# First layer's opening in a written order: rows scaled in pairs on ScalarE, zeros later, routing and sends ahead of the first batch's convolutions

## The chip, the cores and the metric

The kernel runs on one core of a Trainium2 chip. A core has five engines that run their own instruction streams and wait for each other through semaphores: TensorE (PE in the profile; its weight loads are shown apart as PEld), VectorE (DVE), ScalarE (ACT), GpSimd (POOL) and SyncE (SP, which here only issues DMAs). Sixteen DMA engines move data between the off-chip memory and the on-chip memory. The metric is the device time of one execution in microseconds (us), the median of several runs.

## The reference, cut to what matters

The input is 8 batches of 512 rows of 256 numbers in float32, 4096 rows in all. There are two layers, each of the form "normalise, then add an attention-like part and a mixture of experts":

```
xn = layernorm(x)
x  = x + mamba(xn) + experts8_top1(xn)        # first layer
xn = layernorm(x)
x  = x + attention16(xn) + experts8_top2(xn)  # second layer
```

The part called mamba here projects xn to z, x, B, C and dt, makes dt = softplus(dt + bias), runs a 4-tap convolution with silu over x, B and C, runs a state-space recurrence in chunks of 128 rows, forwards and backwards in time (16 heads of 64 channels: 8 per direction), gates with silu(z), normalises and projects back. The first layer's experts: logits = xn·Wr + br, softmax over 8, each row goes to its best expert (relu(row·W1 + b1)·W2 + b2) and is scaled by that probability. The second layer has a latent attention with 16 heads of 16 and a top-2 mixture with limited capacity.

## The kernel before, in words

**Rows in (lines 379 to 403, `steps`, with `norm_and_project`, 128 to 157).** For each batch b of 512 rows (4 tiles of 128): SP asks for u; VectorE makes mean and variance of each tile (`bn_stats`, `bn_aggr`, lines 135 and 136), an inverse square root out of eleven small instructions (`rsqrt`, 162 to 169), and writes the scaled rows to xn (line 141). TensorE turns them (line 148, eight transposes of 128x128), ScalarE copies the result out of PSUM (line 149, twice 128x512), TensorE projects to 24 columns, 16 of dt and 8 logits (line 153, 16 matmuls), and VectorE copies these to proj (line 157). The transposed batch is stored to memory (`xtd`, line 379) and loaded again where the convolutions want it. Only two buffers hold u. In between, ScalarE's queue issues eight DMAs that write zeros into xd0 (line 122), the list of expert rows. Then follow softplus (lines 404 to 425, VectorE mostly), the first batch's convolutions, the decays and the first chunk's matrices. All this is written before `manual_schedule`, so that the framework puts it in an order of its own.

**The chunk loop (from line 1193).** 64 chunks: 8 per batch, four forwards and four backwards in turn. From here each engine takes its instructions exactly in the order in which the program writes them. A chunk does a segment matrix (`segments`, line 1043 on TensorE, exponentials on ScalarE), `pairs`, `weigh` (line 1075, one large VectorE product, once per chunk: a good marker), `inside`, `before`, `behind`, and it carries pieces of the next batch's projections (line 856) and convolutions (lines 865 to 874) and of the last batch's gate and output (line 1000).

**Filler steps.** Between these pieces the loop calls `fill`, which takes one step of a list of generators: four steps per chunk, one more in the first two chunks of each batch and in the last twelve. First comes `route0` (lines 428 to 481): softmax, best expert, ranks, slots, then 32 sends, each a GpSimd DMA that scatters the 128 rows of one tile to their slots in xd0 (line 473, two sends per step). It has 22 steps, all that chunks 0 to 4 offer. Then `blocks`, the first layer's expert matmuls: 39 blocks of 128 rows, 196 steps (weights fetched by GpSimd DMAs, line 539; matmuls in lines 587 and 608). When these are used up, `late` begins: it prepares the second layer. For each batch: `norm` (fetch the first layer's rows, add the experts' rows with an accumulating DMA, normalise in place on ScalarE, line 672, after a DMA at line 665 has stored the rows as they were), `turn` (transpose and project, lines 688 to 701 and 246 to 282) and, over groups of batches, `route` (top 2 and sends of 8-byte pairs, line 762). `norm` of a batch can only begin when the chunk loop has finished that batch.

**The end of the loop and the second layer.** After chunk 63 the last batch is gated, normalised and projected in a short stretch in which `fill` is called 16 times more. Then the attention runs in 128 steps (scores line 1468, exponentials 1483, transposes 1490, values 1499) with the second layer's experts between them; what is left of `late` runs in its first steps: one step ahead of it, four at the end of step 0 (`follow`, line 1594), four in each step from step 1 on.

**A stray DMA of the loop.** At the end of chunk 3 ScalarE's queue clears the second layer's table (`tab`, line 1241, elements of 8 bytes).

## Time and profile before

| | us |
|---|---|
| median of 3 runs | 2028.68 |
| the runs | 2027.3, 2028.68, 2041.08 |
| the profiled execution | 2044.14 |
| its span, first to last instruction | 2042.4 |
| proj of the last batch copied (line 157) | at 84.5 |
| first `weigh` done | at 142.6 |
| `weigh` of chunk 5, of chunk 6 begins | at 219.8, at 240.4 |
| first expert matmul (line 587) | at 232.5 |
| `weigh` of chunk 63 begins | at 1107.0 |
| first scores of the attention (line 1468) | at 1164.4 |

Over the whole span TensorE is busy 88%, VectorE 71%, ScalarE 57%, GpSimd 33%. The share hides that the stretches differ: in the second layer and in most of the chunk loop TensorE is busy nearly all the time at the full granted clock, at the beginning and around the change of layers it is not. The granted clock is the share of TensorE's full clock that the chip allowed in a stretch. A row of the table of stretches gives, for each engine, the busy time and in brackets the number of instructions.

### The profile page before, as it was taken

Reading aid. Unit: us, or ns where it says so; the run is one execution under the profiler, and the core shown is the slowest. Engines: PE = TensorE matmul, PEld = TensorE weight load, DVE = VectorE, ACT = ScalarE, POOL = GpSimd, SP = SyncE. Lnnn points to the kernel's source line nnn. Section 1 sums busy time; section 2 is a strip of 40 time slices with the busy share of each in tenths; the row PEclk is TensorE's granted clock in tenths of the full one; section 3 lists DMA queues with packets and bytes.
Section 4 is the critical chain, followed back from the end, with each engine's and each line's share of the span. In section 5 each row is a group of like instructions: output and inputs, shape, how many; then the busy total and the mean of one; then the engine's idle time right before and its main releaser. Section 6 shows DMA issues by size and latency. Waiting matters only on the chain.

```text
span 2042.4 us, 33668 instructions
## 1 busy us (share of the span) xinstructions
PE 1807.4 (88%) x11768; PEld 1219.7 (60%) x11768; DVE 1440.6 (71%) x3387; ACT 1163.6 (57%) x2552; POOL 680.2 (33%) x619
## 2 busy tenths in 40 slices
PE   4665699899999999997888878999999999999997
PEld 3423477676667777674455545666666666666654
DVE  4685476767667576776746448788888878787885
ACT  1143253544445454453543247888888878788886
POOL 0037465645646564553324442111111111111030
PEclk9987899999999999998888768999999999999999
DMA  8214765454645555446454323231313131314171
GB/s 247 83 42 67 175 209 163 161 182 149 201 161 189 173 171 184 161 133 160 123 156 134 101 79 100 44 105 44 105 45 103 46 98 41 104 40 112 37 136 52
DMA packets 146472, 245.88 MB, mean 120 GB/s; under 512 B 26333, under 2 KB 106079, under 8 KB 134400
## 3 DMA queue, kind: packets, MB, share of 16 engines
q1 hardware_dynamic: 103536, 122.94, 19.5%
q0 software_dynamic: 33392, 114.95, 19.5%
q10 hardware_dynamic: 9376, 5.84, 1.5%
q8 instruction: 94, 1.54, 0.3%
q14 instruction: 74, 0.61, 0.1%
HBM read 184.70 MB, written 59.90 MB: 120 GB/s over the span
## 4 chain that ended last, share of the span: by engine, by line
PE 35%; ACT 10%; DVE 5%; DMA 2%; issue 1%; SPq 0%; ACTq 0%; POOL 0%; DVEq 0%; POOLq 0%
PE p_ps L1490 8%; PE o_ps L1499 6%; ACT s L1483 6%; PE s_ps L1468 4%; PE e_hp L1318 4%; PE e_yp L1331 4%; ACT pT L1491 3%; PE qp L261 2%; DMA xr<-yt 1%; DVE s L1475 1%; DVE s L1473 1%; PE pj L856 1%; PE op L1000 1%; PE fin L1431 1%; PE vp L279 1%
## 5 line engine op out<-in xcount | busy, mean ns | idle before, releaser
L1473 DVE TENSOR_SCALAR s<-s_ps 128x512 f32<-128x512 f32 x512 | 317.8, 682 | 152.5 <-PE s_ps L1468 150.9
L1483 ACT ACTIVATE s<-s,ng 128x512 f32<-128x512 f32 x512 | 330.8, 717 | 0.0
L1475 DVE CUSTOM_DVE_ANT_0 s<-s,band 128x512 f32<-128x512 f32 x512 | 322.7, 684 | 0.0
L1491 ACT COPY pT<-p_ps 128x512 f32<-128x512 f32 x512 | 275.5, 588 | 75.0 <-PE p_ps L1490 68.2
L1490 PE MATMUL p_ps<-ident,s 128*128 128x128 f32 x2048 | 284.5, 282 | 24.2 <-ACT pT L1491 17.9
L1490 PEld LDWEIGHTS p_ps<-ident,s 128*128 128x128 f32 x2048 | 234.0, 143 | 99.5 <-ACT pT L1491 34.4
L1338 POOL DMA_INDIRECT x<-e_yo,slots x28 | 45.6, 1628 | 623.3 <-ACT e_yo L1337 623.3
L856 PE MATMUL pj<-xT,w_in 128*128 128x512 f32 x384 | 204.6, 660 | 16.6 <-DVE cv L869 9.9
L587 PEld LDWEIGHTS h_ps<-xdT,w 128*128 128x128 f32 x1248 | 150.3, 194 | 23.0 <-issue 22.0
L1468 PE MATMUL s_ps<-kT,qT 16*128 16x512 f32 x1024 | 156.9, 664 | 5.2 <-DMA qT<-qd 5.2
L587 PE MATMUL h_ps<-xdT,w 128*128 128x128 f32 x1248 | 153.9, 277 | 3.5 <-DMA w<-in_w_dram,w_idx 3.5
L1027 POOL TENSOR_TENSOR au<-da,half 128x512 f32<-128x512 f32 x64 | 77.0, 1203 | 226.6 <-DVE da L425 107.2
L869 DVE SCALAR_TENSOR_TENSOR cv<-pj,w_conv_w,cv 128x511 f32<-128x511 f32 (+2 forms) x192 | 143.0, 745 | 10.9 <-ACT cv L865 6.9
L608 PE MATMUL y_ps<-w,hT 128*128 128x256 f32 x624 | 147.5, 380 | 0.0
L608 PEld LDWEIGHTS y_ps<-w,hT 128*128 128x128 f32 x624 | 115.7, 190 | 31.9 <-issue 16.9
L856 PEld LDWEIGHTS pj<-xT,w_in 128*128 128x128 f32 x384 | 72.9, 207 | 102.2 <-issue 89.6
L1499 PE MATMUL o_ps<-pT,vt 128*32 128x256 f32 x2048 | 130.9, 396 | 0.1
L1318 PE MATMUL e_hp<-e_xdT,e_w 128*128 128x256 f32 x448 | 121.2, 393 | 8.6 <-ACT e_hT L1321 7.6
L1101 POOL TENSOR_TENSOR yT<-yT,ex 128x512 f32<-128x512 f32 (+1 forms) x48 | 58.6, 1220 | 208.3 <-DVE ex L1100 137.8
L1081 PE MATMUL yd<-mt,xdt 128*64 128x128 f32 x1024 | 76.7, 296 | 44.5 <-DVE mt L1075 44.5
L1331 PE MATMUL e_yp<-e_w,e_hT 128*128 128x256 f32 x448 | 113.5, 386 | 1.0 <-ACT e_hT L1321 1.0
L1499 PEld LDWEIGHTS o_ps<-pT,vt 128*32 128x32 f32 x2048 | 62.1, 113 | 87.2 <-issue 55.1
(296 smaller groups left out, 3080.3 us busy)
## 6 DMA issues: line engine op xcount, KB each, us to landing
ex<-exd SPq DMA_DIRECT2D x96, 128.0 KB
u<-in_u_dram SPq DMA_DIRECT2D x16, 512.0 KB
fr<-fdd SPq DMA_DIRECT2D x64, 128.0 KB
od<-os SPq DMA_DIRECT2D x28, 256.0 KB
e_w<-in_ei_dram SPq DMA_DIRECT2D x7, 1024.0 KB
e_w<-in_eo_dram SPq DMA_DIRECT2D x7, 1024.0 KB
xd<-xd SPq DMA_DIRECT2D x39, 129.0 KB
vd<-vt SPq DMA_DIRECT2D x16, 288.0 KB
```

The lines of the kernel that those rows point to most:

```text
L587: T.matmul(hp[:, i, :], w1[:, k * FF + f * P : k * FF + (f + 1) * P], xdT[:, k * P : (k + 1) * P], start=(k == 0), stop=(k == KC - 1),)
L608: T.matmul(yp, hT[f // 4][:, f % 4, :], w2[:, f * DM : (f + 1) * DM], start=(f == 0), stop=(f == FC - 1))
L856: T.matmul(pj, w_in[:, k, o * P : (o + 1) * P], self.xT[:, k, :], start=(k == 0), stop=(k == KC - 1))
L1318: T.matmul(hp, w1[:, k, f * P : (f + 1) * P], xdT[:, k, :], start=(k == 0), stop=(k == KC - 1))
L1331: T.matmul(yp, hT[:, f, c * P : (c + 1) * P], w2[:, f, :], start=(f == 0), stop=(f == FC - 1))
L1468: T.matmul(sp[i], self.q[r, cols], self.k[r, :], start=True, stop=True)
L1473: V.tensor_scalar(self.p[i], sp[i], -CLAMP, CLAMP, ALU.max, ALU.min)
L1475: V.tensor_tensor_reduce(out=self.p[i], in0=self.p[i], in1=band[:, at : at + S], scale=1.0, scalar=-3.0e38, op0=ALU.mult, op1=ALU.max, acc ...
L1483: A.activation(self.p[i], self.p[i], AF.Exp, bias=self.ng[:, i : i + 1])
L1490: T.transpose(pp[:, k, :], self.p[i][:, k * P : (k + 1) * P], ident)
L1491: A.copy(pT[i][:, :, cc * P : (cc + 1) * P], pp)
L1499: T.matmul(op[32 * i : 32 * i + 32, half * 2 * P : (half + 1) * 2 * P], self.v[:, k, h * (AD + 1) : h * (AD + 1) + 32], pT[i][:, k, :], st ...
```

## The change

The opening moves into the hand-written order, and its parts are put in another sequence.

- All of u is asked for at once, into buffers that are free until later; the batches are taken in pairs, 2 and 3 first, 0 and 1 last, so that the transposed batches 0 and 1 stay on chip and are neither stored nor loaded.
- A pair's 8 tiles share one `rsqrt`. The rows are scaled on ScalarE (`activation` with Identity, a scale and a bias per row) and proj is copied by ScalarE, both on VectorE before.
- The zeros are issued from SP's queue in the second pair, no longer from ScalarE's queue from the first batch on. A row of xd0 and xn is 272 numbers wide, not 258.
- softplus takes a fused instruction per coefficient, where there were two.
- All of `route0` (now 39 steps, one send per step) runs ahead of the loop: the choice of slots before softplus is finished, nine sends before the decays, the other 23 between the first batch's convolution pieces. The loop's filler steps begin with `blocks`.
- w_out is loaded in chunk 2 and scaled in chunk 3. The stray clearing of `tab` stays at the end of chunk 3.
- In `norm` the store of the rows is issued ahead of the statistics (for the last batch already in `output`); in the attention the four steps at the end of step 0 are dropped.

```diff
-DW = DM + 2
+DW = DM + 16
...
-    us = {}
-
-    def ask(b):
-        us[b] = m1.tile([P, TPB, DM], FP, name="u", tag="u", bufs=2)
-        Y.dma_start(out=us[b], in_=rows_of(t["u"], b))
-
-    ask(0)
+    us = []
+    order = [*range(2, B), 0, 1]
+
+    def ask():
+        pool, tag, bufs = ((m1, "z", 1), (m2, "yT", 2), (m2, "yT", 2), (m2, "bc", 2))[len(us)]
+        both = pool.tile([P, HC, S], FP, name=tag, tag=tag, bufs=bufs).rearrange("p k s -> p (k s)")
+        us.append(both.rearrange("p (t d) -> p t d", d=DM))
+        for k in range(2):
+            Y.dma_start(
+                out=us[-1][:, k * TPB : (k + 1) * TPB, :], in_=rows_of(t["u"], order[2 * len(us) - 2 + k])
+            )
+
+    ask()
     w_small = load("w_small", [P, KC, 2 * NH + NE], l0c)
-    ask(1)
+    ask(), ask(), ask()
...
+    def rows_in():
+
+        G2 = 2 * TPB
+        for u, b0 in zip(us, order[::2]):
+            both = (b0, b0 + 1)
+            mv = r0p.tile([P, G2, 2], FP, name="mv", tag="mv")
+            for i in range(G2):
+                st = r0p.tile([P, 6], FP, name="st", tag="st", bufs=4)
+                V.bn_stats(st, u[:, i, :])
+                V.bn_aggr(mv[:, i, :], st)
+            ve = r0p.tile([P, G2], FP, name="ve", tag="ve")
+            V.tensor_scalar(ve, mv[:, :, 1], EPS, None, ALU.add)
+            rs = rsqrt(r0p, ve, [P, G2])
+            nm = r0p.tile([P, G2], FP, name="nm", tag="nm")
+            V.scalar_tensor_tensor(nm, mv[:, :, 0], -1.0, rs, ALU.mult, ALU.mult)
+            for i in range(G2):
+                A.activation(
+                    xn[:, b0 * TPB + i, :DM], u[:, i, :], AF.Identity,
+                    bias=nm[:, i : i + 1], scale=rs[:, i : i + 1],
+                )
+            if b0 == order[0]:
                 Y.dma_start(out=w_in, in_=t["w_in"])
...
+            if b0 == order[2]:
+                n = NBLK // B + 1
+                for k in range(B):
+                    lo, hi = k * n, min(NBLK, (k + 1) * n)
+                    Y.dma_start(
+                        out=xd0.rearrange("(p r) d -> p r d", p=P)[:, lo:hi, :],
+                        in_=bc(blank, 1, [P, hi - lo, DW]),
+                    )
+            xTs = {}
+            for b in both:
+                xTs[b] = m2.tile([P, KC, S], FP, name="xT", tag="xT")
+                for k in range(KC):
+                    tp = bank("tp", [P, S], 0)
+                    for c in range(TPB):
+                        T.transpose(tp[:, c * P : (c + 1) * P], xn[:, b * TPB + c, k * P : (k + 1) * P], ident)
+                    A.copy(xTs[b][:, k, :], tp)
+            for b in both:
+                pp = bank("pp", [P, TPB, 2 * NH + NE], 1)
+                for c in range(TPB):
+                    for k in range(KC):
+                        T.matmul(
+                            pp[:, c, :], xTs[b][:, k, c * P : (c + 1) * P], w_small[:, k, :],
+                            start=(k == 0), stop=(k == KC - 1),
+                        )
+                A.copy(proj[:, b * TPB : (b + 1) * TPB, :], pp)
+                if b > 1:
+                    Y.dma_start(out=xtd[b], in_=xTs[b])
+        return xTs
...
-        V.tensor_scalar(acc, z2, 1.0 / 17.0, 1.0 / 15.0, ALU.mult, ALU.add)
-        for k in range(13, 0, -2):
-            V.tensor_tensor(acc, acc, z2, ALU.mult)
-            V.tensor_scalar(acc, acc, 1.0 / k, None, ALU.add)
-        V.tensor_tensor(acc, acc, z, ALU.mult)
-        V.tensor_scalar(acc, acc, 2.0, None, ALU.mult)
-        V.scalar_tensor_tensor(dt.rearrange(f2), v.rearrange(f2), 0.0, acc.rearrange(f2), ALU.max, ALU.add)
+        V.tensor_scalar(acc, z2, 1.0 / 17.0, None, ALU.mult)
+        for k in range(15, 1, -2):
+            V.scalar_tensor_tensor(acc, acc, 1.0 / k, z2, ALU.add, ALU.mult)
+        V.scalar_tensor_tensor(acc, acc, 1.0, z, ALU.add, ALU.mult)
+        V.tensor_scalar(v, v, 0.0, None, ALU.max)
+        V.scalar_tensor_tensor(dt.rearrange(f2), acc.rearrange(f2), 2.0, v.rearrange(f2), ALU.mult, ALU.add)
...
-            if i % 2:
-                yield
+            yield
...
                     x = asked.pop(b)
+                    Y.dma_start(out=rows_of(x1, b), in_=x)
...
-                Y.dma_start(out=rows_of(x1, b), in_=x)
                 yield
                 if b + 1 in asked:
                     add(b + 1)
...
         with tc.manual_schedule(engines=ENGINES):
+
+            rows, rest, sizes = itertools.chain(route0(), blocks()), late(), step_sizes()
+
+            def send(k):
+                for _ in range(k):
+                    next(rows)
+
+            first, ready = batch[0], rows_in()
+            for b in range(2):
+                batch[b].xT = ready[b]
+            send(1)
+            next(sizes)
+            send(1)
+            pending += [first.x_part(k) for k in range(2)]
+            send(5)
+            next(sizes)
+            send(9)
+            decays()
+            edges()
+            chunk[0].prepare()
+            chunk[1].prepare()
+            chunk[0].segments()
+            chunk[0].cross(range(NH))
+            for k in range(2, 4):
+                slot(lambda: first.x_part(k))
+                send(2)
+            slot(), slot()
+            first.skip()()
+            first.ask(0), first.ask(1)
+            for k in range(4):
+                slot(lambda: first.bc_part(k))
+                send(2)
+                if k == 0:
+                    pending.append(first.start())
+            while pending:
+                slot()
+            send(NTILE - 21)
+            first.tokens(0)(), first.tokens(3)()
+            chunk[0].pairs(first)
+            chunk[0].weigh()
...
+                if n == 2:
+                    Y.dma_start(out=w_out, in_=t["w_out"])
...
                 if late_left:
-                    if n < 1:
-                        last_rows(4)
+                    pass
```

`step_sizes` is the softplus part of `steps` as a generator of two halves; its first half ends behind the two exponentials on ScalarE.

## The prediction

> **What bounds the kernel now.** I read first the page's forty slices of the span (51 us each, busy tenths; PEclk is the granted clock).
>
> ```profile
> PE   4665699899999999997888878999999999999997
> ...
> PEclk9987899999999999998888768999999999999999
> ```
>
> TensorE is full but in two places: the first five slices and the change of layers (slices 19 to 24). Only there can an order be worth anything. Next the table of stretches, cut at the marks of the table above; columns are length, then busy us and instructions of PE, PEld, DVE, ACT, POOL, then granted clock, DMA share, GB/s.
>
> ```profile
> 0.00:84.50 84.50, 45.30 (x193) 40.35 (x194) 39.65 (x211) 10.47 (x18) 3.54 (x22) 1.00 0.62 193
> 84.50:142.60 58.10, 36.54 (x84) 13.71 (x84) 50.74 (x77) 22.92 (x49) 10.12 (x8) 0.79 0.11 35
> 142.60:219.20 76.60, 43.87 (x190) 22.81 (x190) 40.30 (x82) 25.19 (x68) 52.71 (x51) 0.79 0.49 70
> 219.20:240.40 21.20, 13.83 (x62) 9.80 (x63) 9.43 (x14) 3.80 (x9) 11.78 (x12) 0.72 0.83 283
> ...
> 266.60:388.00 121.40, 118.94 (x723) 85.33 (x722) 86.02 (x138) 57.81 (x163) 71.98 (x62) 1.00 0.56 182
> ...
> 912.00:1107.00 195.00, 157.58 (x788) 97.28 (x787) 126.46 (x331) 87.53 (x222) 62.52 (x61) 0.86 0.51 141
> 1107.00:1164.40 57.40, 50.42 (x221) 30.99 (x219) 21.32 (x77) 17.43 (x32) 34.03 (x34) 0.86 0.35 103
> 1164.40:1243.60 79.20, 59.36 (x276) 34.22 (x276) 49.77 (x176) 33.53 (x59) 29.01 (x31) 0.62 0.22 67
> ```
>
> The rows come in within 84.5 us with no engine full. Then VectorE works 50.7 of 58.1 us: softplus and convolutions bound that stretch. Chunks 0 to 4 carry routing and sends: GpSimd has 52.7 of 76.6 us and TensorE only 43.9 at clock 0.79. A steady round of eight chunks takes 121.4 us with TensorE full. Around the end of the loop it is not full again.
>
> How sends hold up chunks 3 and 4 is in the instructions in order of time (start, length, engine, line, and in brackets the idle time and what ended it):
>
> ```profile
> 217.16 0.97 POOL L473 DMA_INDIRECT xd<-xn,slot  x1 [4.98 <-DMA xd<-xn,slot]
> ...
> 219.24 0.69 DVE L1116 TENSOR_TENSOR st<-st,sp 128x512 f32<-128x512 f32 x1 [13.29 <-POOL st L1113]
> ...
> 232.54 3.75 PE L587 MATMUL h_ps<-xdT,w 128*128 128x128 f32 x16 [3.53 <-DMA w<-in_w_dram,w_idx]
> ```
>
> GpSimd waits for earlier sends to land, its product for the state comes late, VectorE idles 13 us for that. The first expert matmul stands at 232.5.
>
> **Rows in.** A pair by the new order: ScalarE scales 8 tiles. The row for that shape on ScalarE is line 672, four in 1.96 to 2.08 us, so 4.0 us. TensorE turns the first batch meanwhile; ScalarE then copies (line 149, two in 1.07 to 1.23) as the second batch is turned (line 148, eight in 1.95 to 2.10): all four copies are out at 7.2, the first batch's two at 5.1. The 32 matmuls of line 153 (16 in 3.67) start when TensorE has turned the second batch, 6.6, and end at 13.9; ScalarE's copy of proj ends at 14.3. It stands ahead of the next pair's scaling, so a pair costs 14.3 and four 57. The first scaling waits for u (4.9 us before), 8 tiles of statistics (four took 1.75, so 3.5), eleven small instructions of 0.2 and two more: 11.5. The rows are in at **68.5**, not 84.5. Zeros, 5.4 MB beside 4.2 of u, 1.6 of w_in and 3.1 of stores, move at 193 to 250 GB/s in 57 to 75 us; the upper end would cost 6 more.
>
> **From there to the loop.** VectorE's list in written order, by its spans in the trace: logits and first softmax part 1.4, dt input 0.7, wait for ScalarE's exponentials 2.0, rest of softmax 1.3, best expert with the rank matmuls 3.8, ranks 5.0, block ends 2.5, slots 2.0; then softplus 13.0 (before 16: seven pairs of 0.68 and 0.42 become seven of 0.66), expert index 1.6, decays 0.8: 34. Then the eight convolution parts at 2.9 (23.2), the start of y 8.6 (four of 0.68 and eight of 0.73), `cbm` and `weigh` 1.6, and waits: 2.5 at the tanh of the first parts, 9 at the detour through memory (fp, four, fs, then 7.75 from fd to the first yT in this trace), 1 for the rest: 46. 68.5 + 34 + 46 = 148.5 against 142.6: **+6**. Ends: the list without waits (65) after a rows-in of 57 gives 122, -21; the list stretched by a quarter (100) after the old 84.5 gives 184.5, +42. I take +6, since each term is a row. The 32 sends lie beside it: 1.28 each on GpSimd, 9 from 87 to 99, the others by 133; what queues behind them there is `au` (needed at 104) and `xdt` (143), not late. The zeros are on SP by then and land before 45.
>
> **Chunks 0 to 5.** They took 97.8 us (142.6 to 240.4). Without sends and with 22 filler steps of expert work: in the steady round five chunks like these take 76.5 (266.6 to 343.1), of which about 10 is the past batch's gate and output (line 1000: four of 1.9 on TensorE, plus squares), so 66 to 68. The first weights must land at chunk 0 in place of chunk 5: 226.0 to 232.5 before, 6. Chunk 5 then costs 14.5, as a steady one. The clearing of `tab` now meets expert weights instead of sends:
>
> ```profile
> 195.00:216.00 21.00, 10.03 (x46) 4.33 (x46) 4.00 (x6) 8.19 (x24) 13.40 (x13) 0.79 1.18 58
> ```
>
> The DMA engines are full at 58 GB/s for 21 us; a steady round wants 182. Weights are asked a block or more ahead (18 us), which covers most; bounds 0 and 21, I take 8, for the fdd detour that stands in it as well. 68 + 6 + 14.5 + 8 = 96.5: **-1**.
>
> **Rest of the loop.** I count filler steps by the code: 282 in the loop, 22 + 196 used for routing and blocks before, so `late` has 64; now 196, so 86. Blocks end at chunk 45 instead of 50. Chunks up to 45 are unchanged. The 22 steps' TensorE work (lines 587 and 608: 153.9 and 147.5 us over 39 blocks of five steps, 1.55 a step, 34 us) has gone forward; five chunks more carry `late`. Chunks with it cost 195/12 = 16.25 against 121.4/8 = 15.2, but start-up (23.0 for one chunk) and the waits for accumulating DMAs come once per batch either way: five times 1, and 2 for each of three chunks where the 32 sends of line 762 now pile on GpSimd, less 4 for emptier last chunks: **+7**; bounds -14 (TensorE work alone) and +20.
>
> **End of the loop.** 57.4 us between the last `weigh` and the first scores hold 35 us of `late` on TensorE (lines 246 to 279, 688, 695) and 32 sends on GpSimd. By my count that work is in the loop now; only the last batch's chain remains: yd, yoff, ex, yT 5.3, gate 4.5, squares, mean and `rsqrt` 6, four outputs 8, loads of q and k 2.4, and some 6 of routing on VectorE: 32. **-25**; bounds -34 and 0 (if the last route fills it).
>
> **Start of the attention.** The chain of waits and ScalarE's rows:
>
> ```profile
> 1173.66 5.21 DMA x<-xr
> ...
> 1178.96 2.08 ACT L672 ACTIVATE xr<-xr,nm,rq_r 128x256 f32<-128x256 f32 x4 [20.07 <-DMA x<-xr]
> ```
>
> The in-place scaling waits for the store just issued, and the four forced steps put it ahead of the first exponentials; TensorE idles 8. The store now comes earlier and the steps are dropped; `late` has 24 steps left there, not 29. I take **-10**, from 8 of idle and 2 of steps; bounds 0 and -20. What is late next is the second layer itself, which is TensorE's.
>
> w_out's scaling (four of 0.35) and the wider rows (5%) I cost at nothing: both lie beside TensorE, in chunk 3 and in DMAs at half load; uncovered, 1.4 and 2.
>
> **Sum.** +6 - 1 + 7 - 25 - 10 = -23. The span 2042.4 becomes 2019.4; the profiled execution (2044.14) lies 15 over the median, and I carry the difference over: 2028.7 - 23 = **2006**.
>
> **Two rules of the Trainium skill that speak against it.** The granted clock is 0.79 where TensorE works 36.5 of 58.1 us. "TensorE: Matmul & The Clock Gate", Part 1, says that an idle window of about 3.4 us brings the clock to half. In the new order TensorE idles through most of 30 us of routing and softplus; at half clock the same 36.5 us would be 58 (estimate from the page), and half of that on the path would make 2016; by the row nothing is added. "SBUF — State Buffer", "SBUF: two separate sides", warns that GpSimd cannot write descriptors while VectorE holds their shared port; sends here took 0.97 to 1.80 beside a busy VectorE, so I leave them.
>
> **Rivals.** (a) As summed, 0.45: 2006, own range 1992 to 2018. (b) The opening comes at its better end and the late chunks go by TensorE's work: -10 and -10 more, 1985; 0.17. For it: TensorE's emptiness above; against: VectorE's list is serial. (c) The gain is spent: late chunks at +20, the end and the attention at half (-17): 2028.7 + 6 - 1 + 20 - 17 = 2037 at worst, with +10 there 2027; 0.25. For it: 195/12 per chunk with TensorE only 81% busy shows that `late` stalls by DMA and GpSimd, not by TensorE. (d) Slower: the written order works in single file. An instruction that waits (ScalarE's proj copy, the detour through fdd, exponentials) holds all behind it, where the framework's order filled gaps; price is the delay of the first `weigh`. Beyond 142.6 + 29 = 172 the change loses, beyond 192 by over 1%; at the far end, 184.5, it gives 2042, and with half of (c) beside it 2052. 0.13. That it does not do what it says is part of (c): fillers that find no batch ready.
>
> **Chances.** 1% is 20 us, about what can be told from no change here. Faster (under 2008): 0.29 of (a) and (b): 0.46. Within: 0.16 of (a), 0.22 of (c), 0.05 of (d): 0.43. Slower, over 2049: the rest of (c) and (d), 0.11. The range 1978 to 2044 leaves out the tail of (b) and the worse half of (d).
>
> **What would show it.** proj complete near 68, first `weigh` near 148, first expert matmul near 160, `weigh` of chunk 6 again near 245, the last near 1119, first scores near 1151, GpSimd without sends in chunks 0 to 4. Wrong it would be through a first `weigh` far from 148, weights that stall chunk 4, or an end of the loop that keeps its 57 us.

## The result, and the profile after

The changed kernel takes **2045.05 us** (median of 11 runs, 2040.11 to 2049.72) beside 2032.21 for the kernel before on the same chip (11 runs, 2021.48 to 2041.08): a ratio of 1.0065, 95% interval 1.0043 to 1.0087. The forecast was 2006 with a range up to 2044. The profiled execution after is 2045.05 us with a span of 2043.4. So the two profiled executions, 2044.14 and 2045.05, differ by 1 us where the medians differ by 13; the paragraph on the base, near the end, comes back to that.

Both profiles at the same marks, in us. "First scores" is here the first record of VectorE's line for the scores. That record is its wait for them: TensorE's first scores, the mark that the prediction used, stand 1.2 us behind it in the kernel before (1164.4) and 3.4 in the kernel after (1175.3), and VectorE's first computing instruction on them at 1166.4 and 1176.5. The "48th record" counts the waits of that line too; it is its 30th or 31st computing instruction, or the wait just before that.

| stretch | before | after | difference |
|---|---|---|---|
| proj complete | 84.7 | 67.8 | -16.9 |
| `weigh` of chunk 0 begins | 140.5 | 151.4 | +10.9 |
| to `weigh` of chunk 6 | 99.9 | 100.5 | +0.6 |
| to `weigh` of chunk 45 | 584.6 | 588.5 | +3.9 |
| to `weigh` of chunk 63 | 282.0 | 294.2 | +12.2 |
| to the first scores | 56.1 | 37.4 | -18.7 |
| to the 48th record of that line | 80.5 | 72.7 | -7.8 |
| to the end | 798.8 | 798.8 | 0.0 |

The forty slices of the kernel after, TensorE's busy tenths and the granted clock:

```profile
PE   6458799999999999969878778999999999999997
...
PEclk9778899999999999979988768999999999999999
```

The early dip has moved: the second to fourth digit (51 to 153 us) were 6, 6, 5 and are 4, 5, 8; the fifth is 7 where it was 6. The dip of the change of layers begins one slice earlier, with a 6 from 868 to 919 us where there was a 9. The stretches of the kernel after, with the columns as in the prediction:

```profile
0.00:67.80 67.80, 45.68 (x193) 40.28 (x194) 24.91 (x122) 27.62 (x57) 4.23 (x24) 1.00 0.66 214
67.80:153.20 85.40, 39.37 (x88) 14.94 (x87) 65.25 (x112) 22.95 (x51) 44.34 (x41) 0.71 0.23 79
153.20:223.90 70.70, 64.78 (x382) 47.62 (x384) 34.05 (x63) 29.33 (x82) 42.60 (x38) 0.91 0.62 169
223.90:251.90 28.00, 16.97 (x88) 10.96 (x84) 11.74 (x20) 6.83 (x20) 8.51 (x7) 0.82 0.69 184
...
839.80:939.10 99.30, 78.59 (x385) 46.46 (x384) 67.17 (x155) 47.98 (x118) 37.11 (x37) 0.86 0.48 132
939.10:1134.50 195.40, 153.07 (x790) 95.95 (x789) 110.11 (x264) 83.66 (x216) 85.02 (x80) 0.88 0.38 108
1134.50:1171.90 37.40, 32.94 (x140) 21.68 (x138) 25.45 (x92) 9.10 (x17) 10.42 (x12) 0.81 0.31 86
1171.90:1244.60 72.70, 56.08 (x277) 33.08 (x277) 47.24 (x161) 33.93 (x61) 21.66 (x24) 0.69 0.23 72
```

Three things are to be seen. The opening behind the rows is now 85.4 us long with VectorE busy for 65.3. Chunks 0 to 5 hold expert matmuls (TensorE 64.8 of 70.7 us), but the step from chunk 5 to 6 takes 28.0 us with TensorE busy for 17. And from chunk 45 to 51 six chunks take 99.3 us with 20.7 of them idle on TensorE. The kernel before had TensorE busy there for 85.9 of 87.5 us:

```profile
824.50:912.00 87.50, 85.89 (x516) 61.35 (x516) 65.03 (x107) 43.90 (x122) 47.46 (x41) 1.00 0.49 156
```

Over the whole way from chunk 45 to 63 TensorE works 231.7 us and is idle for 63.0, where it worked 243.5 and was idle for 39.0 before (the row 912 to 1107 of the prediction added).

**The opening** by VectorE's instructions in time (start, length, and in brackets the idle time and what ended it):

```profile
67.85 0.43 DVE L145 TENSOR_TENSOR pr<-proj,w_br 128x256 f32<-128x256 f32 x1 [35.24 <-ACT proj L396]
71.57 0.42 DVE L152 TENSOR_REDUCE sm_m<-pr 128x32 f32<-128x256 f32 x1 [1.77 <-ACT pr L150]
...
110.22 1.29 DVE L870 SCALAR_TENSOR_TENSOR x<-th,cv 128x512 f32<-128x512 f32 x2 [3.57 <-ACT th L869]
126.88 2.32 DVE L865 SCALAR_TENSOR_TENSOR cv<-pj,w_conv_w,cv 128x511 f32<-128x511 f32 x3 [8.02 <-ACT cv L861]
```

The rows were in at 67.8 as worked out, and the waits are where the forecast looked for them: at the exponentials, the tanh and the detour. In the detour the 8.02 us end with ScalarE's copy behind the products that lead to it; the load from memory itself cost 0.39.

**The jam at chunk 5.** VectorE waits 12.35 us for the piece that makes the detour through memory (line 915):

```profile
244.69 0.69 DVE L915 TENSOR_TENSOR yT<-x,fr 128x512 f32<-128x512 f32 x1 [12.35 <-DMA fr<-fdd]
```

**Chunks 45 to 51.** TensorE's waits from 835 to 1180 us (total, times, longest):

```profile
PE yd L1077 <- DVE mt L1071: 11.5, 5, 3.8
PE yd L1077 <- DVE ve L658: 9.8, 1, 9.8
PE yd L1077 <- DVE proj L696: 9.4, 1, 9.4
PE wp L823 <- DMA w_dn<-in_w_dn_dram: 7.5, 1, 7.5
PE pj L852 <- DVE z L957: 6.8, 1, 6.8
```

Lines 658, 696 and 823 belong to `late`, the second layer's preparation; line 1077 is the chunk's own product, which must wait for `weigh` on VectorE, and `weigh` stands in VectorE's order behind what `late` has written there. In time, on VectorE and TensorE:

```profile
892.62 0.43 DVE L652 BATCH_NORM_STATS2 st<-xr 128x6 f32<-128x256 f32 x1 [7.24 <-DMA xr<-yt]
```
```profile
872.59 1.94 PE L823 MATMUL wp<-w_dn,w_kt 128*128 128x64 f32 x8 [7.54 <-DMA w_dn<-in_w_dn_dram]
897.55 1.98 PE L1077 MATMUL yd<-mt,xdt 128*64 128x128 f32 x16 [9.85 <-DVE ve L658]
```

VectorE waits 7.24 us for the accumulating DMA of the first batch; the chunk's product starts 9.85 us late behind it. And TensorE waits 7.54 us for a weight load that was issued two filler steps before. These two make 17.4 of the 20.7 us of TensorE's idle time there. The wait for the weights is not new: the kernel before has it too, with 7.1 us, five chunks later.

### The profile page after: what moved, and what is told of

Read it like the earlier page. It is cut to its first block, busy times and chain, and to the rows that moved or that the text cites. A ratio compares the mean times of both kernels' runs of the same rounds, so it can differ in the third digit from the quotient of the medians.

```text
span 2043.4 us, 33598 instructions
## 1 busy us (share of the span) xinstructions
PE 1807.3 (88%) x11768; PEld 1226.2 (60%) x11768; DVE 1416.6 (69%) x3296; ACT 1180.8 (58%) x2592; POOL 683.8 (33%) x620
## 4 chain that ended last, share of the span: by engine, by line
PE 60%; DVE 12%; ACT 12%; issue 5%; DMA 4%; POOL 3%; SPq 0%; POOLq 0%; ACTq 0%; DVEq 0%
PE p_ps L1505 7%; PE y_ps L604 6%; PE pj L852 6%; PE h_ps L583 6%; ACT s L1498 6%; PE o_ps L1514 5%; PE e_hp L1333 4%; PE s_ps L1483 4%; PE e_yp L1346 4%; ACT pT L1506 3%; PE op L996 2%; PE seg L1039 2%; PE yd L1077 2%; PE sp L1103 2%; DVE cv L865 1%
## 5 line engine op out<-in xcount | busy, mean ns | idle before, releaser
L852 PE MATMUL pj<-xT,w_in 128*128 128x512 f32 x384 | 199.4, 645 | 18.0 <-DVE cv L865 10.1
L865 DVE SCALAR_TENSOR_TENSOR cv<-pj,w_conv_w,cv 128x511 f32<-128x511 f32 (+2 forms) x192 | 143.2, 746 | 12.5 <-ACT cv L861 8.0
L604 PEld LDWEIGHTS y_ps<-w,hT 128*128 128x128 f32 x624 | 118.2, 194 | 34.9 <-issue 18.7
L852 PEld LDWEIGHTS pj<-xT,w_in 128*128 128x128 f32 x384 | 70.2, 201 | 98.7 <-issue 81.7
L1077 PE MATMUL yd<-mt,xdt 128*64 128x128 f32 x1024 | 77.1, 297 | 42.6 <-DVE mt L1071 23.4
L1052 ACT ACTIVATE mt<-seg,mid 64x64 f32<-64x64 f32 x512 | 109.4, 309 | 0.8
```

Source lines behind the costliest of these rows:

```text
L604: T.matmul(yp, hT[f // 4][:, f % 4, :], w2[:, f * DM : (f + 1) * DM], start=(f == 0), stop=(f == FC - 1))
L852: T.matmul(pj, w_in[:, k, o * P : (o + 1) * P], self.xT[:, k, :], start=(k == 0), stop=(k == KC - 1))
```

## The experiments

The kernel before takes different times on different chips: medians of 2032 (the result), 2043.9, 2041.5, 2066.5, 2064.9 and 2041.1 in the six groups of runs. A ratio is therefore always to the kernel before on the same chip, and across groups the marks inside the profile are compared rather than the totals. Where an expectation speaks of the way from the last `weigh` to the first scores, it means VectorE's mark, 37.4 after.

### Is the reading repeatable?

The kernel before twice more, the changed kernel once more, with nothing edited.

> The kernel before, unchanged, profiled once more, since its eleven times spread from 2021 to 2041 us around a median of 2032 and the profiled one (2044) is above them all. Theory A: the spread sits where the first layer ends, because there the late steps wait for accumulating DMAs and sends; a profile near 2032 has its last weigh (1107.0) and first scores (1163.2) about 12 us earlier, and the first weigh (140.5), the steady round of 121.4 and the stretch behind the first scores unchanged within 2. Rival B: it sits in the opening and chunks 0 to 5, where sends and clearing crowd the DMA engines; then weigh of chunk 6 (240.4) is already 10 earlier. Rival C: it is spread, in proportion to length, by the granted clock: every stage 0.6 percent shorter.

> The kernel before, unchanged, once more with a profile. On a chip like the last one it takes 2065 where the one of the forecast takes 2032. Theory A (the start of the attention, where transfers through memory are waited for, is what differs: 86.1 us there for the changed kernel, 72.7 on the chip of its first profile): on a slow chip the stretch from the first to the 48th score grows by 10 to 15 and the stretches of the loop that wait for DMAs (chunks 0 to 5, the last weigh to the first scores) take the rest; the steady round and the attention behind stay within 3. Rival B: all stretches are longer in proportion. On a chip that takes about 2032 the profile answers instead where 2042 and 2030 part: in the same stretches by A, everywhere by B.

> The changed kernel, unchanged, on the chip of the three that follow, because the kernel before alone took 2032 to 2066 us on the chips so far. Theory A: the ratio to the kernel before is a property of the kernels, 1.004 to 1.009 again. Rival B: the stretches that wait for DMAs differ from chip to chip, and so does the ratio, below 1.000 or above 1.012; then all other ratios are read only beside this one. In either case the profile has the two waits (7.5 and 9.8) and 45 to 63 near 295.

| | first `weigh` begins | to 6 | to 45 | to 63 | to scores | to 48th record | to end | ratio |
|---|---|---|---|---|---|---|---|---|
| before | 140.5 | 99.9 | 584.6 | 282.0 | 56.1 | 80.5 | 798.8 | |
| before_again | 142.0 | 103.0 | 587.7 | 281.9 | 54.2 | 73.5 | 798.2 | 0.9996 (0.9972 to 1.0020) |
| before_third | 141.8 | 100.7 | 583.7 | 278.5 | 56.2 | 80.2 | 801.5 | 1.0005 (0.9971 to 1.0038) |
| after | 151.4 | 100.5 | 588.5 | 294.2 | 37.4 | 72.7 | 798.8 | 1.0065 |
| after_again | 153.1 | 104.7 | 585.1 | 297.3 | 37.3 | 86.1 | 806.0 | 0.9986 (0.9967 to 1.0005) |

The three profiles of the kernel before end between 2040.6 and 2042.5, each made up a little differently: none of theories A, B and C about the spread is shown, since no profile near 2030 came. What repeats is the pattern of the change: +9 to +13 at the first `weigh`, some +15 from chunk 45 to 63, -18 to the first scores. What does not repeat is the sign of the result: on the chip of after_again, where the kernel before takes 2064.9, the changed kernel's 2063.5 are no slower. Rival B of that run, a ratio below 1.000, has the better case, though the interval reaches to 1.0005. The changed kernel's own difference between the two chips is in the start of the attention (13.4) and behind it (7.2). Of the 13.4, TensorE's busy time makes 4.2 (60.28 us in the run on the slower chip, 56.08 in the first), its idle time the rest:

```profile
1177.60:1263.70 86.10, 60.28 (x276) 33.43 (x276) 47.94 (x162) 33.31 (x59) 22.25 (x24) 0.66 0.20 61
```

Whether the kernel before loses its 33 us in the same place on such a chip was not seen; its profiles came from other chips.

### The edits at the end of the loop

In end_only these three edits are made in the kernel before; in end_undone they are taken back in the changed kernel:

```diff
+                    Y.dma_start(out=rows_of(x1, b), in_=x)
...
-                Y.dma_start(out=rows_of(x1, b), in_=x)
...
-                    if c == TPB - 1 and self.b < B - 1:
+                    if c == TPB - 1:
...
-                    if n < 1:
-                        last_rows(4)
+                    pass
```

> The kernel before with only the three edits at the end of the loop (store of the rows ahead of the statistics, the last batch stored in output, the four steps at attention step 0 dropped). Theory A (as I predicted): they carry the start of the attention, -10, and nothing of the loop, so 2022. Rival B (from the trace after, where the stretch between the first score and the 48th became only 7 shorter and the rest none): -4 to -7, 2025 to 2028. Rival C: the work is only put off, the four steps return one by one in later attention steps: 0, 2032.

> The changed kernel with those three edits undone. If they are worth the same in either kernel (theory A), its time is the changed kernel's 2045 plus what the kernel with them alone gains. Rival B: in the changed kernel fewer late steps are left at the end (24, not 29), so they matter less there: within 3 of 2045. Rival C: they cost in the loop what they win in the attention: faster than 2045.

end_only: 2043.15 us, ratio 0.9998 (0.9976 to 1.0020). end_undone: 2054.05, ratio 1.0052 (1.0030 to 1.0074). The idle time that the forecast had shown in front of the transposes (8.1 us before, 7.2 and 8.1 in the two repeats, 8.3 in end_undone) is gone in end_only and in the kernel after. Yet of it only 2 to 4 us arrive: from first scores to the 48th record the mean of three profiles of before is 78.1 and end_only has 75.7; end_undone has 76.8 and the kernel after 72.7. The way from the last `weigh` to the first scores is 4 to 6 us shorter in end_only too (50.3). The medians show no gain from the edits; by the interval of end_only it is less than 5 us either way, so theory A's 10 is refuted, and between rivals B (4 to 7) and C (none) it isn't decided. For end_undone it stays open what they are worth, since the changed kernel itself did not run on that chip. Where the rest of the 8 us goes isn't shown; the next wait, 5.5 us in front of line 215 (246 before), is in all of them.

### The opening and the first chunks

route_loop puts routing and sends back into the filler steps; weights fetches the first two blocks ahead of the loop; clear_flat writes the table in 128 pieces of 224 bytes in place of 3584 of 8; loop_flat is route_loop and clear_flat together.

```diff
 # route_loop
+            def routing():
+                one = route0()
+                for k in range(6 + NTILE // 2):
+                    next(one)
+                    if k == 0 or k >= 6:
+                        next(one)
+                    yield
-            rows, ... = itertools.chain(route0(), blocks()), ...
+            rows, ... = itertools.chain(routing(), blocks()), ...
-            send(...)
...
 # weights
-            send(NTILE - 21)
+            send(NTILE - 21 + 1)
 # clear_flat
+    clean = ctile("clean", [P, NSLOT1 // P, 2])
+    G.memset(clean, 0.0)
+    G.iota(clean[:, :, 0].bitcast(I32), pattern=[[0, NSLOT1 // P]], base=NT, channel_multiplier=1)
...
-                        out=tab.rearrange("(p r) d -> p r d", p=P),
-                        in_=bc(blank[:, DM : DM + 2], 1, [P, NSLOT1 // P, 2]),
+                        out=tab.rearrange("(p r) d -> p (r d)", p=P), in_=clean.rearrange("p r d -> p (r d)")
```

> The changed kernel with routing and sends back in the loop's filler steps (22 steps, two sends each), the rows still scaled by pairs and the rest of the written order kept. Theory A (the written order's single file is the loss: routing, 16 us of VectorE, and its waits stand on the path of the first weigh): first weigh near 134 instead of 151.4, chunks 0 to 5 about 98 as in the kernel before, weigh of chunk 6 near 232 instead of 251.9; with 64 instead of 86 late steps in the loop the late chunks are 12 shorter and the end 17 longer: about 2045 - 20 + 5 = 2030. Rival B (the opening's order is no loss, the late chunks are): weigh of chunk 6 again near 250, and the whole within 5 of 2045. Rival C (VectorE's long list is the same wherever it stands): first weigh 134, but chunks 0 to 5 longer than 98 by as much.

> The changed kernel; the clearing of the second layer's table at the end of chunk 3 writes 128 pieces of 224 bytes from a prepared tile instead of 3584 pieces of 8 bytes. Theory A (the clearing jams the DMA engines, and the first expert weights and the detour through memory wait behind it): the weigh of chunk 5 to that of chunk 6, 28.6 us, shrinks to 16 to 18, chunk 6 begins near 241, and all behind it moves by 10 to 12: ratio 0.995 of the changed kernel, 2034 beside 2045. Rival B (it is the detour through memory itself, or the order of the convolutions): 28 stays. Rival C (chunk 6 comes earlier, but the late steps and the attention take it up again): weigh of chunk 6 near 241, the end within 3 of the changed kernel's.

> The changed kernel; the fetch of the weights and rows of the first two expert blocks is issued right behind the last send, ahead of the first chunk's pairs and weigh, not in the loop's first filler step. Theory A (chunk 1's 23.3 us are the first weights' transfer): weigh of chunk 2 comes 5 to 7 earlier, at 175 instead of 181.3, and the whole gains 5. Rival B (the fetch of the rows has to wait for the last send to land whenever it is issued, and the sends end near 140): under 2 us. Rival C (one step more is taken from the late steps' end: the late chunks grow by one step): no gain in the end.

> Routing and sends as the loop's filler steps, as in the run before of that kind, and the clearing in 128 pieces as well. Theory A (the gain of the opening, 7 us at the first weigh, was spent in chunks 4 and 5 on the clearing, since the same 3584 pieces meet the sends there): chunks 0 to 5 take 88 instead of 105.7, weigh of chunk 6 near 222, and the whole comes to 0.988 of the kernel before, about 2020 on a chip where that takes 2044. Rival B (the sends themselves hold the chunks): chunks 0 to 5 near 98, ratio 0.992. Rival C (whatever is won there is waited for at the change of layers): ratio 0.995 as without.

**clear_flat**: 2032.97 us, ratio 0.9966 (0.9949 to 0.9983). Chunk 5 to 6 takes 15.8 us in place of 28.0, chunk 6 begins at 238.0 in place of 251.9, and the profile ends 12.2 earlier than the first one after: theory A, nearly with its numbers. What it is worth in the medians is less sure, since the changed kernel itself did not run on that chip; `weights`, which differs from it by one step, took 2047.74 there, 14.8 more. The step from chunk 5 to 6 itself repeats: with routing ahead of the loop it takes 25.1 to 31.7 us in all nine profiles with the small pieces, and 15.8 to 16.9 in all four with 128. The stretch from chunk 5 to 6 of that run, and the detour, which VectorE no longer waits for:

```profile
222.20:238.00 15.80, 15.80 (x90) 10.23 (x86) 11.62 (x19) 7.29 (x20) 8.71 (x7) 1.00 0.65 218
```
```profile
230.56 0.68 DVE L918 TENSOR_TENSOR yT<-x,fr 128x512 f32<-128x512 f32 x1
```

How the jam works is in the 16 us from 212 on, first of the kernel after, then of clear_flat:

```profile
212.00:228.00 16.00, 16.00 (x99) 10.27 (x96) 8.11 (x17) 7.83 (x22) 10.36 (x10) 1.00 0.83 27
```
```profile
212.00:228.00 16.00, 16.00 (x106) 10.46 (x105) 6.59 (x15) 7.96 (x24) 11.66 (x11) 1.00 0.71 228
```

The DMA engines are 83% busy for 27 GB/s, or 71% busy for 228. The small pieces are not what fills them: 3600 packets on ScalarE's queue make 30.8% of the engines' time, 22 ns each. The packets of the other queues become long: GpSimd's 82 take 22.7%, 0.7 us each, where in clear_flat 393 take 43.9%, 0.29 each. TensorE is full in both for as long as the blocks in hand last, so the price comes only after these 16 us: it stands still from 236.1 to 247.2.

**weights**: 2047.74 us, ratio 1.0024 (1.0002 to 1.0046). The `weigh` of chunk 2 came at 185.0, not at 175 and not before the 181.3 of the kernel after, so theory A's number isn't there. But the run doesn't decide it, for the first `weigh` itself took 9.75 us in place of 1.75 (148.4 to 158.2), beside GpSimd's products from 149.1 to 157.1; from its end to chunk 2 it is 26.8 us, 28.1 after. The rest of the run moved by a step and is no cleaner.

**route_loop**: 2034.03 us, ratio 0.9951 (0.9929 to 0.9974), on the chip where end_undone had 1.0052. The first `weigh` begins at 134.0, as theory A had it: routing ahead of the loop costs 16 to 17 us there. But chunks 0 to 5 then take 105.7, not 98, so chunk 6 begins at 239.7 and not at 232, which lies between A and rival C. From 45 to 63 it has 286.3 and to the first scores 50.9, near A. Its profiled execution (2045.45) is 11 above its median, so where the rest of the gain lies isn't in it.

**loop_flat**: 2027.95 us, ratio 0.9934 (0.9911 to 0.9958), against 0.9951 without the flat clearing a difference within the intervals. Chunks 0 to 5 take 92.2 in place of 105.7, between theories A and B. The two stretches, route_loop first:

```profile
134.00:239.70 105.70, 62.95 (x252) 34.16 (x253) 58.34 (x104) 31.16 (x86) 64.57 (x62) 0.74 0.51 105
```
```profile
135.10:227.30 92.20, 60.59 (x252) 32.89 (x253) 58.36 (x104) 31.05 (x86) 64.67 (x62) 0.78 0.33 112
```

With the sends in the loop TensorE has no more than 61 to 63 us of work in that time, so it waits even without the clearing.

### The late steps

late_held, late_spread, held_flat and held_flat40 put empty filler steps where `late` would run; late_gaps, gap_w and gap_s put three empty steps between a load and its first use.

```diff
 # late_held (22), held_flat (22, with clear_flat), held_flat40 (40, with clear_flat)
-            rows, rest, sizes = itertools.chain(route0(), blocks()), late(), step_sizes()
+            rows, rest, sizes = itertools.chain(route0(), blocks(), range(22)), late(), step_sizes()
 # late_spread
                     if next(rows, "end") == "end":
-                        next(rest, None)
+                        kept_back[0] += 1
+                        if kept_back[0] % 4 or kept_back[0] > 88:
+                            next(rest, None)
 # gap_w and late_gaps
             Y.dma_start(out=w_dn, in_=t["w_dn"])
-            yield
+            for _ in range(4):
+                yield
 # gap_s and late_gaps
                         add(b)
-                        yield
+                        for _ in range(4):
+                            yield
```

> The changed kernel; between the first layer's blocks and the second layer's preparation 22 empty filler steps are put, so that the preparation begins where it did before (chunk 50) and has 64 steps in the loop. Theory A (moving this work forward only moves its cost): chunks 45 to 63 shrink from 294.7 to about 283 and the way from the last weigh to the first scores grows from 37 to about 49; the whole within 3 of the changed kernel. Rival B (as I predicted: the early start saves the 25 at the end for 7 in the loop): slower by 15 or more. Rival C (the early start costs more than it saves): faster by 5 or more.

> The changed kernel; the second layer's preparation begins as early as there, at chunk 45, but of the filler steps from there on each fourth is left empty until 22 have been. Theory A (each of the 22 steps simply costs more in a chunk, 34 / 22 = 1.55 us, than at the end, 0.6): as with the 22 empty steps in front, 2024 to 2031 where the changed kernel has 2045. Rival B (it is the early start that costs, since the preparation then runs into its own loads and the last block's writes): near 2045; the wait of TensorE for the small weight product (7.5) and that for the statistics of the first batch (9.8) are still there.

> The changed kernel; three empty steps more between the second layer's weight loads and their first use, and three more between the first batch's accumulating DMA and its statistics, six in all. Theory B (two waits on DMAs in the hand-written order, 7.5 and 9.8 us, are the loss): both waits go, chunks 45 to 51 shrink from 99.3 to about 84, the whole gains 12 to 15. Theory A (the number of early steps counts, whichever they are): 6 of 22 steps, a gain of about 6.

> The changed kernel; only the three empty steps between the second layer's weight loads and their first use. Theory A (each of the two waits counts by itself): the wait of 7.5 goes, that of 9.8 stays, a gain of 6 to 8 on the changed kernel. Rival B (one cause alone, the loads: what follows is late only through them): the whole gain of both, 15 or more. Rival C (three steps shift what follows to other places in the chunk, and new waits of that size come): within 3.

> The changed kernel; only the three empty steps between the first batch's accumulating DMA and its statistics. Theory A: the wait of 9.8 goes, that of 7.5 stays, a gain of 8 to 10. Rival B (the loads are the cause): 2 or less. Rival C (the shift alone): within 3 of the changed kernel or to either side by as much as new waits make.

> The changed kernel with the 22 empty filler steps ahead of the second layer's preparation and with the clearing in 128 pieces. The two alone gave 0.9954 and 0.9966 of the kernel before. Theory A (two separate causes, one at chunk 5, one from chunk 45 on): the gains add, 13.9 us at the weigh of chunk 6 and 34 less 13.5 at the change of layers; ratio 0.985. Rival B (both win only time that is then waited for at the change of layers): ratio near 0.995 again.

> As with 22 empty steps and the clearing in 128 pieces, but with 40 empty steps, so that only 46 steps of the preparation run in the loop. Theory A (a step costs 1.55 in a chunk and 0.6 at the end, whatever their number): 18 steps more gain 17 again. Rival C (the end has idle time for some 22 steps only; what is left then stands in front of the first scores): a loss of 10 or more against 22 empty steps, and the way from the last weigh to the first scores grows beyond 65.

| | late steps in the loop | 45 to 63 | 63 to scores | both | median | ratio |
|---|---|---|---|---|---|---|
| before | 64 | 282.0 | 56.1 | 338.1 | 2032.21 | 1 |
| after | 86 | 294.2 | 37.4 | 331.6 | 2045.05 | 1.0065 |
| late_held | 64 | 259.9 | 50.8 | 310.7 | 2031.22 | 0.9954 (0.9936 to 0.9972) |
| late_spread | 64 | 267.6 | 52.6 | 320.2 | 2055.11 | 0.9933 (0.9904 to 0.9962) |
| late_gaps | 86, 6 of them empty | 273.8 | 37.1 | 310.9 | 2035.37 | 0.9839 (0.9790 to 0.9887) |
| gap_w | 86, 3 empty | 289.7 | 35.2 | 324.9 | 2059.93 | 0.9967 (0.9949 to 0.9986) |
| gap_s | 86, 3 empty | 290.8 | 37.6 | 328.4 | 2053.51 | 0.9934 (0.9911 to 0.9958) |
| held_flat | 64 | 261.4 | 60.7 | 322.1 | 2042.33 | 0.9871 (0.9825 to 0.9917) |
| held_flat40 | 46 | 223.4 | 85.7 | 309.1 | 2085.28 | 1.0089 (1.0056 to 1.0122) |

The kernel before has 2041.46 beside late_held, 2064.92 beside gap_w and gap_s (and after_again, 2063.5), 2066.47 beside the others.

**late_held** refutes the forecast of the end: with the 22 steps held back the loop wins 34.3 us and the end gives back 13.4, so that the early start, which I had taken for the gain, costs 21 us between chunk 45 and the first scores. Rival C of that run holds: its 2031.22 stand beside the 2047.74 of `weights` on the same chip, the changed kernel but for one step.

**late_gaps** begins `late` as early as the kernel after, and six empty steps give 310.9 in sum, as 22 steps held back give 310.7. Chunks 45 to 51 take 83.3 (843.9 to 927.2; 84 expected), and the two waits are no longer among TensorE's longest:

```profile
843.90:927.20 83.30, 68.86 (x358) 39.88 (x357) 65.58 (x133) 42.74 (x108) 38.89 (x36) 0.92 0.43 116
927.20:1117.70 190.50, 164.90 (x816) 102.16 (x814) 117.90 (x287) 87.72 (x223) 87.60 (x81) 0.88 0.45 129
```
```profile
PE yd L1079 <- DVE mt L1073: 11.3, 5, 3.6
PE pp L692 <- ACT xT L686: 7.6, 6, 4.0
```

So the early start need not cost these 20 us, and what it cost was idle time of TensorE: 63.0 us between chunk 45 and 63 after, 40.0 here, with nearly the same work (231.7 and 233.8). That the two waits alone are the cause isn't shown. Of the 23.0 us less idle time only 6.3 lie in chunks 45 to 51. There VectorE still waits 3.3 us for the accumulating DMA, and other waits come, 14.4 us in all. What else the chunks lose there is work that moved behind chunk 51 (358 matmul records in place of 385) and a higher granted clock (0.92, not 0.86). The other 16.7 us lie behind chunk 51, where the six steps have shifted everything against the chunks. And late_spread, which keeps the early start and adds no gap, has both waits still: TensorE's 7.4 us for the weights, VectorE's 8.6 for the accumulating DMA, with 8.0 of TensorE behind it. Yet its sum lies in the middle (320.2), so that 22 steps fewer in the loop, spread out, win 11.4 us with both waits in place. In the medians late_gaps is 31 us below the kernel before on its chip, where 12 to 15 below the changed kernel was expected; the changed kernel itself did not run there.

**gap_w and gap_s** take the waits one at a time. Beside after_again on the same chip the medians fall by 3.6 and by 10.0 us; 6 to 8 and 8 to 10 were expected. The marks between 45 and 63 fall by 7.6 (gap_w) and 6.5 (gap_s). Each takes away its own wait; in gap_w VectorE still waits 6.0 us for the accumulating DMA, and TensorE's wait behind it is 5.2, not 7.4 as in after_again. TensorE's idle time between the marks falls from 64.9 to 49.0 (gap_w) and 49.5 (gap_s). Its waits of the chunk's product for VectorE, under whatever instruction's name, make 27.2 us in after_again, 18.3 in gap_w and 20.0 in gap_s (the second line is the load's wait that stays):

```profile
PE yd L1079 <- DVE mt L1073: 20.0, 6, 6.5
PE wp L825 <- DMA w_dn<-in_w_dn_dram: 8.2, 1, 8.2
```

With both gaps the product's wait is 11.3 (late_gaps) and 9.4 (gaps_flat below), and the idle time 40.0 and 41.5. So the single gains in the marks (14.1) are less than what both bring there (18.7 from after_again to gaps_flat, 20.4 from the kernel after to late_gaps), and in idle time more (31.3 against 23.4). Why they don't add up wasn't followed further.

**held_flat40** bounds the other side. With 46 late steps in the loop the sum is lowest, 309.1, but the second layer starts without its rows:

```profile
826.50:1049.80 223.30, 183.03 (x985) 110.37 (x983) 165.51 (x314) 111.56 (x294) 89.43 (x81) 0.94 0.39 108
1049.80:1135.50 85.70, 47.45 (x218) 28.46 (x216) 35.60 (x134) 20.06 (x38) 37.43 (x38) 0.77 0.44 119
1135.50:1260.80 125.30, 87.73 (x361) 49.59 (x362) 49.86 (x167) 41.88 (x74) 23.69 (x26) 0.62 0.19 61
```

From first scores to the 48th record it takes 125.3 us where held_flat on the same chip takes 93.4, and what follows 826.2 where that takes 799.9. The median is 43 us longer: rival C. The end has room for some 22 steps, not for 40.

**held_flat** adds two mends and has 0.9871, where 0.985 was expected if they add: within its interval. Its marks show both in the loop (89.8 for chunks 0 to 5, 261.4 from 45 to 63); the way to the first scores is 10 longer than in late_held, on another chip, and that wasn't followed.

### Both mends together, in either kernel

gaps_flat is the changed kernel with both gaps and the flat clearing; before_fixed is the kernel before with the same (the gap behind the weight loads one step longer).

> The changed kernel with both gaps of three empty steps and the clearing in 128 pieces. Theory A (the clearing's jam and the two waits are separate): 13 at the weigh of chunk 6 and 15 to 20 between 45 and 63, together 28 to 33 below the changed kernel on this chip, 0.98 of the kernel before or less. Rival B (the change of layers takes it up): 15 to 18 below the changed kernel.

> The kernel before with the two mends tried on the changed one: the clearing in 128 pieces and empty steps (four and three, seven in all) between the weight loads and their use and between the first accumulating DMA and its statistics. Theory A (the mends are worth the same in either kernel and the change by itself nothing): 0.978 of the kernel before, as the changed kernel with them. Rival B (the early jam meets sends here, which hide it, and of the two late waits only that for the weights, 7.1 us, is there): 0.990 to 0.995, so that the change with the mends is worth 1.2 to 1.7 percent. Rival C: no gain at all, 0.998 to 1.002.

gaps_flat takes **2020.62 us** where the kernel before takes 2064.92 and the changed one 2063.5: ratio 0.9772 (0.9745 to 0.9800). Its chunks 0 to 5 and its change of layers:

```profile
152.30:242.10 89.80, 81.05 (x471) 57.72 (x472) 47.35 (x83) 37.18 (x104) 53.94 (x47) 0.94 0.57 191
824.60:1103.10 278.50, 237.04 (x1173) 144.03 (x1171) 183.50 (x417) 130.32 (x331) 125.39 (x116) 0.88 0.44 123
1103.10:1140.30 37.20, 29.05 (x136) 19.98 (x136) 24.57 (x93) 10.54 (x20) 11.31 (x12) 0.86 0.32 87
```

Against after_again chunks 0 to 5 are 14.9 shorter and 45 to 63 are 18.7 shorter: 33.6 of the 48.2 between the two profiles. Theory A said 28 to 33; the medians differ by 43, more than it said. Of the rest 8.0 us lie behind the 48th record, where nothing was changed.

before_fixed takes 2014.54 us where the kernel before takes 2041.06: ratio 0.9852 (0.9807 to 0.9896). Chunks 0 to 5 fall to 92.6, 45 to 63 to 251.0, the way to the first scores stays 56.1. So the mends are worth 26.5 us without the change: theory A's 0.978 and rival B's 0.990 to 0.995 both miss. Between 45 and 63 they bring 27 to 31 us here, though of the two late waits TensorE had only that for the weights (7.1), and chunks 6 to 45 take 592.3, 5 to 9 more than in the three profiles of before. With the gaps went other waits of TensorE too, above all those of line 1064 for VectorE (15.6 us in four before, 0.2 here). So the empty steps do more than take away the two waits; what else they do wasn't followed. Set side by side, 0.9772 and 0.9852 give the change with the mends 0.8%; since the two ratios come from different chips, and the change alone had 1.0065 on one and 0.9986 on another, that much isn't shown.

## Why the prediction was wrong

**The sum.** Of the 39 us between 2006 and 2045, 24 are the terms of the sum and 15 the base. Forecast was -23 on the span; the profile pair gives +1.0. Each term by its own marks (the prediction's, so TensorE's record at the scores):

| term | forecast | measured | miss |
|---|---|---|---|
| first `weigh` done (142.6) | +6 | 153.2: +10.6 | +4.6 |
| chunks 0 to 5 (97.8) | -1 | 98.7: +0.9 | +1.9 |
| rest of the loop (866.6) | +7 | 882.6: +16.0 | +9.0 |
| end of the loop (57.4) | -25 | 40.8: -16.6 | +8.4 |
| start of the attention (79.2) | -10 | 69.3: -9.9 | +0.1 |

**Rest of the loop and its end, the steps that failed.** The forecast priced five more chunks with `late` at 1 us each plus three times 2 for sends, less 4, from the mean of the chunks that had carried it (195/12), and took the 25 us at the end as the return. Measured are +16.0 and -16.6.

Of the 16.0 us 3.9 lie before chunk 45, where the forecast had nothing; the kernel before alone spreads by 4.0 there (583.7 to 587.7). From 45 to 63 it is +12.2: TensorE works 11.8 us less than before, near the bound of -14 that the forecast gave for its work alone, but is idle for 24.0 more. A mean over chunks hides such idle time. The early steps met their own loads: 7.5 us for the weights, 9.8 us for the first batch's rows. I had read the wait for accumulating DMAs in the trace of before and written that it comes "once per batch either way"; where it falls in the chunk makes the difference, because `weigh` stands behind it. That the idle time can be avoided is shown: late_gaps took 20 us out of this stretch (294.2 to 273.8) by six empty steps and nothing else, and late_held comes to the same sum. That it is these two waits alone isn't: late_spread has both and wins 11.4 us with 22 steps fewer in the loop, and before_fixed wins 27 to 31 where only one of them stood. How the rest comes about stays open.

The end kept 40.8 us where 32 was worked out. The forecast said that the 35 us that TensorE spent on `late` there would be in the loop by then, so that only the last batch's chain remained. Not all of it was: between the last `weigh` and the first scores TensorE still has 12.6 us of it (lines 215, 230, 239, 248, 684 and 691).

**The opening.** The rows were in at 67.8 against 68.5 forecast. The 80 us from there to the first `weigh` were 85.4. Routing, softplus and decays took 33.1, not 34; what follows took 52.2, not 46. Of these 6 us nearly 4 are the start of y: its twelve instructions took 12.4 us, not 8.6. Beside GpSimd's products (143.8 to 150.6) they took 1.41 to 1.53 us each, the others 0.68 to 0.75. The trace of before had that already (11.2 us), and the forecast priced all twelve by the fast ones. The waits of that part came to 15.3 where 12.5 were listed. The term's sign and its mechanism stand, its size was 4.6 too small. Rival (d) is this effect, priced from 172 on, and 153 is far from it. route_loop shows what the order costs at this mark (17 us); at chunk 6 it is still 12 (251.9 against 239.7), with 22 filler steps of expert work done in exchange. The softplus, the wider rows and the scaling of w_out had no run of their own.

**Chunks 0 to 5.** The sum came out near, from other parts: the five chunks took 70.7, not 74, and the jam at `tab` cost 28.0 less 15.8, so 12 and not 8 (clear_flat). The sentence "weights are asked a block or more ahead, which covers most" was too kind: TensorE's blocks lasted until 236.1, 24 us after the clearing was issued at 212.0, and the detour through memory had no cover. "DMA: Bandwidth & Descriptors" of the Trainium skill, "Why small descriptors are slow (HBM only)", says that each piece carries a fixed cost. The runs agree in the rate, 27 GB/s at 83% against 228 at 71%, and show besides that the packets of the other queues became long, 0.7 us for GpSimd's in place of 0.29.

**Start of the attention.** Right by its marks (-9.9), and still not to be relied on: the three edits alone bring 0.9998 in the medians, and the stretch takes 72.7 on one chip and 86.1 on another in the same kernel.

**The base.** I carried the profile's 2044 over to the median of three runs, 2028.7, as a constant 15. Six medians of the kernel before lie between 2032 and 2066, so the three runs stood below all of them, and there is no constant: the profile after lies on its median. On the span alone, 2042.4 - 23 + 1.7, I would have said 2021; wrong too, by the terms above. The 13 us of the result are 1 by the two profiles, -1.4 between the medians on another chip. That the change is slower by 0.65% holds on the chip of the result; on that of after_again it isn't (0.9967 to 1.0005).

**The rivals.** Rival (c), "the gain is spent", is nearest to what happened: late chunks +16 of the +20 named, but the end and the attention gave -26.5, more than its half (-17). Its sum, +8 at worst, is nearer to the measured +1 than the -23. It put the loss down to stalls by DMA and GpSimd, and stalls it was; that they could be avoided by six steps it didn't see.

**The two rules weighed.** The clock in the opening fell to 0.71 from 0.79 with TensorE busy for 39.4 of 85.4 us; the first `weigh` came 4.6 later than without a price for that, where half clock on the path was put at 10. No run separates it. Sends beside a busy VectorE were no hold-up: the opening's last send is out before 140 and nothing on the way to `weigh` waits for it. What did hold VectorE up was GpSimd's arithmetic beside it, as the start of y shows, and that stood in no term.

## What to carry to other kernels

In an order written by hand, bringing work forward can lose as much as it gains if what it waits for isn't brought forward as well: look up for each moved step the DMA that it needs, and count the steps between request and use, not the engine time. An instruction that waits for a DMA on VectorE holds all that stands behind it, here the one product that TensorE needs next (7.24 us on VectorE, 9.85 on TensorE). Six empty steps between request and use brought some 20 us between chunk 45 and 63, more than the whole rearrangement, though it isn't shown to be by these waits alone. Price an instruction by the rows that have the same neighbours, not by the fastest. And before a difference of under 1% is forecast, take the base from as many runs and chips as the result will have.

## What the runs showed of the hardware

- From chip to chip the times differ by more than the change: in six groups of runs the same kernel has medians from 2032 to 2066 us, and the ratio of two kernels went from 1.0065 to 0.9986. Of the 26.3 us between two profiles of the changed kernel 20.6 lie from the first scores on, with the same 4727 DMA packets in the start of the attention; TensorE's waits there grow by idle time that the profile calls "issue" (4.9 us at the scores, none on the other chip).
- Writing 28 KB in 3584 pieces of 8 bytes cost the changed kernel 12 us. In the kernel after 99% of these pieces had ended by 222.8, but GpSimd's packets of 2 KB and more still took 1.3 us on average from 225 to 229, 0.9 from 229 to 233 and 0.3 from 233 to 245. The same bytes in 128 pieces left chunk 5 at 15.8 us with TensorE full.
- In the opening VectorE and GpSimd slowed each other when both computed: from 143.8 to 150.6 in the kernel after VectorE's instructions of line 922 took 1.41 to 1.53 us, 0.74 to 0.75 before that, and GpSimd's products 1.48 us, 1.04 at 154.0 with VectorE idle. Sends of GpSimd (0.97 us and more each) did not do this.
- Single edits in an order written by hand don't add up: the two gaps bring 7.6 and 6.5 us alone between chunk 45 and 63, 18.7 together (with the flat clearing); in TensorE's idle time 15.9 and 15.4 alone, 23.4 together.
